# Layer 2's gathers and scatters: one at each of four points of a step, rows fetched two groups ahead, stores a step later, g_init inside VectorE's product

## The chip, the core and the metric

The kernel runs on one core of a Trainium2 chip. Five engines work from their own in-order queues: PE (matrix products), DVE (elementwise work and reductions), ACT (activations and copies), POOL (elementwise work, and here the issue of every indirect DMA) and SP (which issues the plain DMAs). The metric is the time of one execution in microseconds (us); lower is better.

## What is computed

The input x has 32 sequences of 128 tokens with 128 features. Four layers follow; each adds a gated cross-attention over a context and a gated feed-forward part. What the change touches is the end of layer 1 (a mixture of experts), the whole of layer 2, and a preparation for layer 3 that runs beside layer 2:

```python
    # end of layer 1: top-2 mixture over 8 experts, on t = rmsnorm(x1, g2)
    x = x + tanh(g_ffn[1]) * _L1_ffn_ref(_layernorm(x), ...)
    # layer 2: attention, 8 heads of 16; then a top-2 mixture with LayerNorm
    x = x + tanh(g_xattn[2]) * _L2_xattn_ref(ctx_2048, _layernorm(x), mask, b)
    x = x + tanh(g_ffn[2]) * _L2_ffn_ref(_layernorm(x), gamma, beta, Wg, ...)
    # layer 3, the part prepared beside layer 2: a decayed running sum of
    h_patch = rmsnorm(ctx_2048, g_init)[..., :128]      # then picked by patch ends, + h
```

The top-2 mixture is computed by sending: each token's row is stored twice, once into a slot of each of its two experts; each expert works through its slots; each token's two result rows are fetched back, weighted and added to x.

## The kernel before, in words

The 32 sequences are eight groups of four (NG = 8, NB = 4). x stays in SBUF for the whole run as eight tiles of 128 tokens by 4 x 128.

**Stages.** The attention of layers 0, 1 and 1f (the small attention inside layer 1's feed-forward part) runs in one pipeline, up to about 1257 us of the profiled execution. The experts of layer 1 follow, up to 1416. Then layer 2's attention, up to about 1791. Then layer 2's experts, and from about 1987 layer 3.

**A step.** Attention is cut into steps (`Pipe.turn`, lines 434 to 454). Layer 2 has four a group: two sets of four heads, each in two halves of two sequences. A step traces, in this order: the row maxima put into the query stack and the finishing of older outputs (lines 439 to 441); the weights of the part that is four back (`self.todo[0][0]()`, scores transposed and their exponential); the products with the values of the part before that, and at a group's last part its `after`; then

```python
            move(to_fetch, 3)
            move(to_store, 2)
```

(lines 450, 451); then one piece of the oldest `after` in the queue `afters`, if there was one when the step began; then one piece of the work beside (`last_layer`, line 1167). After the step, `run` (line 410) takes one piece of the next group's `before`.

**before(g)** (line 1251) empties `to_fetch`, adds the fetched rows (`routes1.add`, line 833: eight products per group on DVE), takes a LayerNorm (POOL computes the inverse root, line 208), and ends its first piece. Its second piece makes the query parts (line 289: two casts on POOL, lines 301 and 303) and the values (POOL, lines 285, 286), and queues the fetch of the following group's rows: eight indirect DMAs of 128 rows, issued on POOL (line 821), into one of two buffers `got`.

**after(g)** (line 1265) adds the attention's output, takes a LayerNorm with a second scale (POOL, line 254: `w`), and ends its first piece. Further pieces: the router's logits and the top-2 choice (`Routes.take`, line 642, two yields); the last piece appends eight stores to `to_store` (line 705), each an indirect DMA on POOL (line 636) which needs the slot numbers (`slot_r`, line 692). So an `after` has four pieces and a group has four steps. In layer 1f a group has eight steps, its `after` has five pieces, and it uses the same `take` and the same `turn`.

**last_layer** computes, group by group, the root mean square of the context (POOL line 208), multiplies it in on DVE (line 1197) and multiplies by the row `g_init` on POOL (line 1198), before a product with the decay matrix on PE (line 1203).

**flush** (line 456) runs the steps that are left; then, while there are `afters`, it takes a piece of one and a piece of the work beside. `drain` then empties `to_store`.

**Order.** What the program text says is not the order on the engines. The builder's planner lines up each engine's instructions by when it reckons their inputs and buffers to be ready; text order is their priority. An indirect DMA of this kernel is in addition marked with `keep_in_program_order`, which ties it behind the instruction traced before it on POOL. Once lined up, each engine's queue is fixed and runs in order.

Of the kernel before, what the change touches and what calls it, by code (L numbers as in the profile page):

```python
# [22 lines left out]
P = 128  # L23
# [49 lines left out]
def tile_flamingo_gated(  # L73
# [149 lines left out]
    def bc(a, n=D):  # L223
        return a[:, :, None].to_broadcast([a.shape[0], a.shape[1], n])
# [15 lines left out]
                of = of.rearrange("p (h e d) -> p e h d", e=2, d=8)  # L240
            nc.vector.tensor_scalar(to, of, mv[:, b, 0:1], r[:, b : b + 1], ALU.subtract, ALU.mult)  # L241

    def layernorm(pool, a, tag="y", bufs=None, halves=False, again=None):

        mv = moments(pool, a)
        if again:

            w = pool.tile([P, 2, NB], F32, tag="w2", name="w2")  # L250
            nc.vector.tensor_scalar(w[:, 0], mv[:, :, 1], EPS, None, ALU.add)
            nc.vector.tensor_scalar(w[:, 1], mv[:, :, 1], 1.0 + EPS, EPS * EPS, ALU.mult, ALU.add)
            w2 = w.rearrange("p i b -> p (i b)")
            nc.gpsimd.tensor_tensor(w2, w2, m05.to_broadcast([P, 2 * NB]), ALU.pow)
            r, r2 = w[:, 0], w[:, 1]
        else:
            r = rsqrt(pool, mv[:, :, 1])
        y = None
        if tag:
            y = pool.tile([P, NB, D], F32, tag=tag, name="y", bufs=bufs)  # L260
            scaled(y, a, mv, r, halves)
        if not again:
            return y
        h = pool.tile([P, NB, D], F32, tag=again, name="h")
        scaled(h, a, mv, r2)
        return y, h

# [125 lines left out]
    def move(queue, n=None):  # L393
        for do in queue[:n]:
            do()
        del queue[:n]

    class Pipe:


# [33 lines left out]
        def turn(self, ahead):  # L434
            self.place.append(to_place[:])
            to_place.clear()
            place = self.place.pop(0)
            ready = bool(self.afters)
            for do in to_finish + place:
                do()  # L440
            to_finish.clear()
            if len(self.todo) > ahead:
                self.todo[0][0]()
            if self.last:
                _, products, after = self.last
                products()
                if after:
                    self.afters.append(after())
            self.last = self.todo.pop(0) if len(self.todo) > ahead else None
            move(to_fetch, 3)  # L450
            move(to_store, 2)
            if ready:
                self.advance(self.afters)
            self.beside()

        def flush(self):
            while self.todo or self.last:
                self.turn(0)
            for do in to_finish:
                do()  # L460
            to_finish.clear()
            while self.afters:
                self.advance(self.afters)
                self.beside()

        def drain(self):
            self.flush()
# [141 lines left out]
    class Routes:  # L609
# [32 lines left out]
        def take(self, pool, psum, g, logits, rows, gate, eps):  # L642
# [52 lines left out]
            if eps:  # L695
# [3 lines left out]
                self.weight[:, g], tops, gates[:, gate : gate + 1], den[:, None, :].to_broadcast([P, 2, NB]),  # L699
                ALU.mult, ALU.mult,  # L700
            )
            yield
            for b in range(NB):
                for k in range(2):
# [415 lines left out]
    with ExitStack() as outer:  # L1120
# [29 lines left out]
        with ExitStack() as stack:  # L1150
# [16 lines left out]
            def last_layer():  # L1167
# [13 lines left out]
                for g in range(NG):  # L1181
                    bs = slice(g * NB, (g + 1) * NB)
                    hot = pool.tile([P, NB, P], BF, tag="hot", name="hot", bufs=1)
                    nc.vector.tensor_tensor(
                        hot, CST(cst, "iota_s")[:, None, :].to_broadcast([P, NB, P]), bc(ends[:, bs], P), ALU.is_equal,
                    )
                    ck = pool.tile([P, NB, D], F32, tag="ck", name="ck", bufs=1)
                    nc.sync.dma_start(out=ck, in_=ctx_all[bs, :, 0:D].rearrange("b s d -> s b d"))
                    cnt = psum.tile([P, NB], F32, tag="tp", name="cnt")
                    for b in range(NB):  # L1190
                        nc.tensor.matmul(
                            cnt[:, b : b + 1], lhsT=hot[:, b, :], rhs=ones_b[:, 0:1], start=True, stop=True
                        )
                    nc.vector.tensor_scalar(bound[:, bs], cnt, 1.0, None, ALU.min)

                    r = rms_scale(pool, ck, values_of(pool, g))
                    nc.vector.tensor_tensor(ck, ck, bc(r), ALU.mult)
                    nc.gpsimd.tensor_tensor(
                        ck, ck, ROW(row, "g_init")[:, None, :].to_broadcast([P, NB, D]), ALU.mult
                    )  # L1200
                    yield
                    pd = psum.tile([P, NB, D], F32, tag="tp", name="pd")
                    nc.tensor.matmul(flat(pd), lhsT=CST(cst, "decay"), rhs=flat(ck), start=True, stop=True)
                    dep = pool.tile([P, NB, D], F32, tag="dep", name="dep", bufs=1)
                    nc.scalar.copy(dep, pd)

                    pg = psum.tile([P, NB, P], F32, tag="tp", name="pg")
                    for b in range(NB):
                        at = g * NB + b
                        nc.tensor.matmul(  # L1210
                            pg[:, b, :], lhsT=bound[:, at : at + 1].to_broadcast([P, P]), rhs=CBF(cbf, "tri"),
                            start=True, stop=True,
                        )
                    pick = pool.tile([P, NB, P], F32, tag="pick", name="pick", bufs=1)
                    nc.vector.tensor_scalar(flat(pick), flat(pg), -1.0, 0.0, ALU.add, ALU.max)
                    nc.vector.tensor_scalar(flat(pick), flat(pick), float(P - 1), iota_p, ALU.min, ALU.is_equal)
                    yield
                    po = psum.tile([P, NB, D], F32, tag="tp", name="pdp")
                    with_bias(po, "b_in")
                    for b in range(NB):  # L1220
                        nc.tensor.matmul(
                            po[:, b, :], lhsT=pick[:, b, :], rhs=dep[:, b, :], start=False, stop=b == NB - 1,
                            skip_group_check=True,
                        )
                    nc.scalar.copy(dep, po)
                    nc.sync.dma_start(out=depool[g], in_=flat(dep))
                    yield
# [22 lines left out]

            def before(g):
                if g == 0:
                    gots[0] = routes1.fetch(pool, 0)
                move(to_fetch)
                routes1.add(g, gots.pop(g))
                y = layernorm(pool, xs[g], halves=True)
                yield
# [1 line left out]
                va = augmented(pool, values_of(pool, g), 8, 16, "va", nc.gpsimd.tensor_copy)  # L1259
                o = pool.tile([P, NB, D], F32, tag="o", name="o", bufs=3)  # L1260
                at2[g] = q, [ctx_keys[g]], [va], o
                if g + 1 < NG:
                    gots[g + 1] = routes1.fetch(pool, g + 1)

            def after(g):
                add_gated(xs[g], 2, at2.pop(g)[-1])
                y, yn = layernorm(pool, xs[g], tag="y2", bufs=1, again="yn")
                add_gated(xs[g], 6, y)
                yield
                fT = pool.tile([P, NB, P], F32, tag="fT", name="fT", bufs=1)  # L1270
# [267 lines left out]
```

## Time and profile before

| | |
|---|---|
| median of 4 runs | 2203.02 us (2199.84 to 2214.75) |
| the profiled execution's own time | 2206.84 us |
| its span, first to last instruction | 2205.1 us |
| layers 0, 1, 1f with the stores of layer 1 | up to 1256.6 us |
| layer 2's first fetch | 1419.1 us |
| layer 2's last store issued | 1788.6 us |
| indirect fetches in layer 2's attention | 64, of 1006 ns mean on POOL |
| indirect stores in layer 2's attention | 64, of 989 ns mean on POOL |
| POOL's product with g_init | 8, of 1312 ns mean |

The profile is of one execution. A line of groups gives the source line, the engine, the operation, the tiles, the count, the busy time and the mean, and after the bar the idle time of that engine just before such instructions and what ended it. A view of waits says which engine's instruction waited for which, the total, how often, and the longest. The chain of waits follows the work that ended last back from the end of a stretch, and gives each line's share. A timeline has the start, the duration, the engine and line, and in brackets the idle time ahead of the instruction.

### The profile page before, as it was taken

What the parts mean: (1) busy time and instruction counts of PE and PEld (TensorE: products, weight loads), DVE (VectorE), ACT (ScalarE), POOL (GpSimd) and SP (SyncE); (2) the same over time, 40 slices, a digit from 0 to 9 for tenths busy, and PEclk for the clock granted to TensorE, in tenths of its full rate; (3) what the DMA queues carried; (4) which work ended last, traced back from release to release, by engine and by line L of the source; (5) the groups of instructions that cost most, each with busy time, mean ns of one, the idle gap of its engine ahead of it and who ended that gap; (6) DMA issues with size and microseconds to landing.
All of it is one profiled execution on the core that took longest, in us unless ns stands there. A gap on an engine that the chain in (4) does not pass through costs nothing.

```text
span 2205.1 us, 35468 instructions
## 1 busy us (share of the span) xinstructions
PE 1664.3 (75%) x13624; PEld 1007.4 (46%) x13624; DVE 1207.2 (55%) x3480; ACT 894.5 (41%) x1110; POOL 647.8 (29%) x645
## 2 busy tenths in 40 slices
PE   0699998989999999788877399645656549992445
PEld 0454445456666666555445244333534424441223
DVE  7645455375645577677666333366657621113677
ACT  0277565656778655333233133211112114430335
POOL 5101101010100013355554580254554320006430
PEclk9999999999999999977888599867677669995576
DMA  6564558534323342211211144344343123332110
GB/s 207 154 231 161 188 200 274 183 100 126 100 84 100 104 120 73 54 53 53 59 51 48 60 152 150 113 117 136 104 122 116 33 91 122 132 110 72 32 36 19
DMA packets 164536, 244.66 MB, mean 111 GB/s; under 512 B 20560, under 2 KB 102288, under 8 KB 164112
## 3 DMA queue, kind: packets, MB, share of 16 engines
q1 hardware_dynamic: 156176, 225.62, 33.0%
q0 software_dynamic: 8192, 16.79, 2.5%
q8 instruction: 107, 1.75, 0.3%
q14 instruction: 61, 0.50, 0.1%
HBM read 139.74 MB, written 101.24 MB: 109 GB/s over the span
## 4 chain that ended last, share of the span: by engine, by line
PE 39%; POOL 14%; DVE 14%; issue 7%; DMA 3%; ACT 2%; SPq 0%; POOLq 0%; DVEq 0%; ACTq 0%
PE ye L786 5%; POOL got L821 5%; PE av L581 4%; PE ph L1294 4%; POOL by_expert_r L636 4%; PE sct L498 4%; PE sc L498 3%; PE ph L969 3%; PE p L1135 2%; PE tpe L773 2%; PE p L1137 2%; DVE mx L529 1%; DMA got<-by_expert_r,slot_r 1%; PE tp L272 1%; POOL r L208 1%
## 5 line engine op out<-in xcount | busy, mean ns | idle before, releaser
L564 ACT ACTIVATE w<-sct 128x1024 f32<-128x1024 f32 x288 | 292.6, 1024 | 340.1 <-PE sct L498 337.7
L529 DVE TENSOR_REDUCE mx<-sc 128x8 f32<-128x1024 f32 x160 | 194.8, 1219 | 122.6 <-PE sc L498 122.2
L498 PEld LDWEIGHTS <-stack_q 96*128 96x128 bf16 x2560 | 193.1, 109 | 134.3 <-issue 104.6
L821 POOL DMA_INDIRECT got<-by_expert_r,slot_r x128 | 126.7, 990 | 337.6 <-issue 336.5
L534 DVE TENSOR_REDUCE mx<-sc 128x4 f32<-128x1024 f32 x128 | 152.9, 1221 | 132.7 <-PE sc L498 132.2
L581 PE MATMUL av<-w,va 128*9 128x128 f32 (+2 forms) x3584 | 203.2, 295 | 28.1 <-POOL w L567 24.5
L498 PE MATMUL sc<-stack_k,stack_q 96*128 96x128 bf16 x1536 | 144.9, 241 | 51.5 <-DVE mx L529 21.3
L498 PE MATMUL sct<-stack_q,stack_k 128*128 128x128 bf16 (+1 forms) x1536 | 142.7, 237 | 23.7 <-DVE mx L529 15.4
L498 PEld LDWEIGHTS <-stack_k 128*128 128x128 bf16 (+1 forms) x1536 | 112.1, 107 | 79.5 <-issue 76.4
L301 POOL CAST hml<-whole 128x512 bf16<-128x512 f32 (+1 forms) x56 | 37.2, 664 | 352.2 <-ACT whole L300 177.4
L581 PEld LDWEIGHTS av<-w,va 128*9 128x9 f32 (+2 forms) x3584 | 99.8, 94 | 79.7 <-POOL w L567 36.5
L786 PE MATMUL ye<-hid,w 128*128 128x512 f32 x276 | 133.4, 593 | 1.5 <-DVE hid L1140 1.5
L969 PE MATMUL ph<-h,w 128*128 128x512 f32 x256 | 122.7, 606 | 1.8 <-ACT hn L972 0.9
L208 POOL TENSOR_TENSOR r<-r,m 128x4 f32<-128x4 f32 x56 | 57.4, 1025 | 219.6 <-DVE r L207 211.9
L969 PE MATMUL ph<-hn,w 128*128 128x512 f32 x256 | 121.2, 604 | 0.7 <-ACT hn L972 0.7
L498 PE MATMUL sc<-stack_l,stack_q 96*128 96x128 bf16 x1024 | 111.2, 239 | 0.0
L587 ACT COPY ot<-av 128x512 f32<-128x512 f32 x112 | 65.4, 584 | 102.2 <-PE av L581 95.1
L567 POOL TENSOR_SCALAR_AFFINE_SELECT w<-w 128x1024 f32<-128x1024 f32 x64 | 70.6, 1105 | 110.5 <-ACT w L564 110.2
L498 PE MATMUL sct<-stack_q,stack_l 128*128 128x128 bf16 x1024 | 99.0, 235 | 3.3 <-DVE mx L529 3.3
L564 ACT ACT_TABLE_LOAD x72 | 92.4, 1283 | 9.7 <-PE sct L498 8.5
L593 PE MATMUL tpo<-cst,ot 128*128 128x128 f32 x448 | 81.0, 303 | 17.5 <-DVE mrows L550 9.8
L241 DVE TENSOR_SCALAR y<-x,bmv,r 128x128 f32<-128x128 f32 x160 | 48.6, 360 | 73.9 <-POOL r L208 72.0
(288 smaller groups left out, 3312.6 us busy)
## 6 DMA issues: line engine op xcount, KB each, us to landing
by_expert_r<-zeros SPq DMA_DIRECT2D x40, 1024.0 KB
stack_q<-q SPq DMA_DIRECT2D x96, 288.0 KB
stack_k<-k SPq DMA_DIRECT2D x96, 288.0 KB
k<-hml SPq DMA_DIRECT2D x16, 1152.0 KB
w<-in_e_dram SPq DMA_DIRECT2D x23, 514.5 KB
xt<-by_expert_r SPq DMA_DIRECT2D x46, 256.0 KB
by_expert_r<-yt SPq DMA_DIRECT2D x46, 256.0 KB
q<-hml SPq DMA_DIRECT2D x72, 128.0 KB
```

What stands on the lines that cost most here:

```text
L208: nc.gpsimd.tensor_tensor(r, r, m05.to_broadcast([P, NB]), ALU.pow)
L498: nc.tensor.matmul(dst[:, h * P : (h + 1) * P], lhsT=stat[rows, 4 * e + h, b], rhs=mov[rows, 4 * e + h, b], start=start and h == e == 0, s ...
L529: nc.vector.tensor_reduce(mx[:, :, b0 : b0 + 2].rearrange("p h b -> p b h"), sc.rearrange("p i (h k) -> p i h k", h=4), AX.X, ALU.max, neg ...
L534: nc.vector.tensor_reduce(mx[:, :, b0], sc.rearrange("p i (h k) -> p h i k", h=4), AX.XY, ALU.max, negate=True,)
L564: nc.scalar.activation(w.rearrange("p i h k -> p i (h k)"), sc, AF.Exp)
L581: nc.tensor.matmul(av[32 * h : 32 * h + dv + 1, b * P : (b + 1) * P], lhsT=values[c][:, b, 4 * u + h, :], rhs=w[:, i, h, :], start=c == 0, ...
L593: nc.tensor.transpose(tp[:, b].rearrange("p s r -> p (s r)"), ot[:, b, :], ident)
L636: ins = nc.gpsimd.indirect_dma_start(out=self.rows(), out_offset=bass.IndirectOffsetOnAxis(ap=slots, axis=0), in_=rows, in_offset=None,)
L786: nc.tensor.matmul(y, lhsT=w2[:, f, :], rhs=hid[:, f, :], start=f == 0, stop=f == n_f - 1)
L821: ins = nc.gpsimd.indirect_dma_start(out=got[:, k, b, :], out_offset=None, in_=self.rows(), in_offset=bass.IndirectOffsetOnAxis(ap=self.sl ...
L969: nc.tensor.matmul(ph, lhsT=wt[:, c, f * P : (f + 1) * P], rhs=h[:, c, :], start=c == 0, stop=c == 3)
L1294: nc.tensor.matmul(ph, lhsT=E2(w, "w1")[:, f * P : (f + 1) * P], rhs=xT, start=True, stop=True)
```

## The change

- `turn` no longer moves three fetches and two stores together. A new `drip` moves one of the two queues by one; it is called at four points of a step: after the placing, after the weights, after the products and `after`, and at the end. Odd calls prefer a fetch, even ones a store; an empty queue gives its turn to the other. `flush` calls it twice for each piece of an `after` that it takes. Since `turn` is shared, the stores of layer 1f move this way too.
- `take` has one more yield ahead of appending the stores. An `after` of layer 2 has five pieces now, one of layer 1f six.
- Layer 2 fetches rows two groups ahead, into three buffers: group 0's and group 1's at the start, then group g + 2's from `before(g)`. The tile `yn`, from which rows are stored, has three buffers instead of two.
- `last_layer` multiplies by the root mean square and by g_init in one DVE instruction for each of four sequences; POOL's product is gone.

```diff
+    turns = [0]
+    def drip():
+        turns[0] += 1
+        first, other = (to_fetch, to_store) if turns[0] % 2 else (to_store, to_fetch)
+        move(first or other, 1)
...
             to_finish.clear()
+            drip()
             if len(self.todo) > ahead:
                 self.todo[0][0]()
+            drip()
             if self.last:
                 _, products, after = self.last
                 products()
                 if after:
                     self.afters.append(after())
             self.last = self.todo.pop(0) if len(self.todo) > ahead else None
-            move(to_fetch, 3)
-            move(to_store, 2)
+            drip()
             if ready:
                 self.advance(self.afters)
             self.beside()
+            drip()
...
             while self.afters:
                 self.advance(self.afters)
                 self.beside()
+                drip()
+                drip()
...
             yield
+            yield
             for b in range(NB):
                 for k in range(2):
                     to_store.append(...)
...
-                    nc.vector.tensor_tensor(ck, ck, bc(r), ALU.mult)
-                    nc.gpsimd.tensor_tensor(
-                        ck, ck, ROW(row, "g_init")[:, None, :].to_broadcast([P, NB, D]), ALU.mult
-                    )
+                    for b in range(NB):
+                        nc.vector.scalar_tensor_tensor(
+                            ck[:, b, :], ck[:, b, :], r[:, b : b + 1], ROW(row, "g_init"), ALU.mult, ALU.mult
+                        )
...
             def before(g):
                 if g == 0:
-                    gots[0] = routes1.fetch(pool, 0)
-                move(to_fetch)
+                    gots[0] = routes1.fetch(pool, 0, 3)
+                    move(to_fetch)
                 routes1.add(g, gots.pop(g))
...
-                if g + 1 < NG:
-                    gots[g + 1] = routes1.fetch(pool, g + 1)
+                if g == 0:
+                    gots[1] = routes1.fetch(pool, 1, 3)
+                move(to_fetch)
+                if g + 2 < NG:
+                    gots[g + 2] = routes1.fetch(pool, g + 2, 3)
...
-                y, yn = layernorm(pool, xs[g], tag="y2", bufs=1, again="yn")
+                y, yn = layernorm(pool, xs[g], tag="y2", bufs=1, again="yn", again_bufs=3)
```

## The prediction, made before the result was known

> **What bounds the kernel now.** I read the page first, for the engines' shares and the chain that ended last.
>
> ```profile
> span 2205.1 us, 35468 instructions
> PE 1664.3 (75%) x13624; PEld 1007.4 (46%) x13624; DVE 1207.2 (55%) x3480; ACT 894.5 (41%) x1110; POOL 647.8 (29%) x645
> PE ye L786 5%; POOL got L821 5%; PE av L581 4%; PE ph L1294 4%; POOL by_expert_r L636 4%; PE sct L498 4%; PE sc L498 3%; PE ph L969 3%; PE p L1135 2%; PE tpe L773 2%; PE p L1137 2%; DVE mx L529 1%; DMA got<-by_expert_r,slot_r 1%; PE tp L272 1%; POOL r L208 1%
> ```
>
> POOL is busy only 29% of the span, yet its issues of fetches (L821) and stores (L636) hold 9% of the chain. The change acts where they are issued, so I cut layer 2's attention into head, body and tail (busy time by engine, then granted clock, DMA share, GB/s):
>
> ```profile
> 1416.00:1463.00 47.00, 6.80 (x46) 5.32 (x46) 23.38 (x81) 1.19 (x2) 32.16 (x35) 0.52 0.34 98
> 1463.00:1735.00 272.00, 168.79 (x1676) 130.37 (x1677) 178.55 (x698) 50.52 (x69) 125.30 (x131) 0.72 0.39 115
> 1735.00:1797.00 62.00, 21.10 (x208) 15.98 (x207) 28.05 (x141) 6.92 (x11) 26.57 (x26) 0.56 0.15 51
> ```
>
> In the body PE is busy for 169 of 272 us, DVE for 179, POOL for 125. No engine is full: the body is bound by hand-overs between queues. The chain from 1560 to 1665 says which, and DVE's waits in the body and the groups of layer 2's attention give prices:
>
> ```profile
> by line: DMA got<-by_expert_r,slot_r 17.1%; issue 10.0%; POOL by_expert_r L636 8.6%; POOL got L821 7.9%; DVE bst L218 6.0%; POOL w L254 4.8%; POOL r L208 3.9%; POOL ck L1198 3.6%; DVE mx L529 3.2%; DVE y L241 2.9%; DVE h L241 2.9%; PE pdp L
> ...
> DVE x L833 <- DMA got<-by_expert_r,slot_r: 20.3, 12, 4.2
> DVE y L241 <- POOL r L208: 17.5, 5, 6.2
> DVE y L241 <- POOL w L254: 11.3, 6, 4.6
> DVE ck L1197 <- POOL r L208: 5.2, 6, 1.2
> ...
> L833 DVE SCALAR_TENSOR_TENSOR x<-got,weight_r,x 128x128 f32<-128x128 f32 x64 | 22.5, 365 | 27.6 <-DMA got<-by_expert_r,slot_r 27.5
> L1198 POOL TENSOR_TENSOR ck<-ck,row 128x512 f32<-128x512 f32 x8 | 10.5, 1312 | 5.9 <-DVE ck L1197 3.3 <-DVE r L207 1.7 <-DVE bound L1194 0.9
> L1197 DVE TENSOR_TENSOR ck<-ck,r 128x512 f32<-128x512 f32 x8 | 5.9, 740 | 6.1 <-POOL r L208 6.1
> ```
>
> A third of that stretch of chain is a fetch landing, a fetch issued or a store issued. POOL's timeline shows the queueing:
>
> ```profile
> 1648.98 0.97 POOL L821 DMA_INDIRECT got<-by_expert_r,slot_r  x1 [0.30 <-DMA stack_k<-k]
> 1650.26 0.96 POOL L821 DMA_INDIRECT got<-by_expert_r,slot_r  x1 [0.30 <-issue]
> 1651.52 1.00 POOL L636 DMA_INDIRECT by_expert_r<-h,slot_r  x1 [0.30 <-issue]
> 1652.83 0.98 POOL L636 DMA_INDIRECT by_expert_r<-h,slot_r  x1 [0.30 <-issue]
> 1653.84 1.05 POOL L208 TENSOR_TENSOR r<-r,m 128x4 f32<-128x4 f32 x1
> ```
>
> Eleven indirect DMAs run back to back from 1639.4, one each 1.28 us (0.97 and a gap of 0.30); the inverse root for a LayerNorm stands behind them, and DVE waits 6.2 us for it. The program text hands out five DMAs a step; the planner has made eleven of it.
>
> **The change, part by part**, against the profiled execution's own 2206.84 us (span 2205.1 and 1.7 around it), which is 3.8 above the median of the runs.
>
> *Rows fetched two groups ahead.* Removed: DVE's 20.3 us of waits in the body. The other 7.2 of the 27.5 lie in the head, where group 0's rows have nothing ahead of them, and stay. Bounds: all 20.3, or none. None is possible because the adds already run early: the rows of group 6 are added from 1585 to 1605, while the text puts them after a step of group 5 that takes its maxima at 1645. The planner issues an add as soon as it reckons the row landed, and a third buffer lets it do so earlier still. A wait that goes is also partly replaced: DVE idles a third of the body anyway. I take 0.4, -8.
>
> *The issue of those DMAs.* Count and price stay (64 fetches, 64 stores in layer 2), but a lone DMA ahead of an inverse root delays it by at most 1.28. DVE's wait for L208 without a queue is 5.2 / 6 = 0.87; five waits should cost 4.3 and cost 17.5, so 13.2 is queue. For L254, without the 4.6 at 1724.8 which belongs to the tail, 6.7 in five, less 4.3, is 2.4. Queue: 15.6. All of it may go (-15.6). The other end is a gain turned round: fetch and store now alternate, so a fetch and a root may stand behind a store that waits for its slot (POOL stood 31.6 us in four such waits in the body), +10 for one more of the mean 7.9 and a little. The planner bunches again, so I take a third, -5. The new fetch also precedes its add by some three steps, 30 us, so a late fetch itself costs nothing as long as that lead is there; without it the 20.3 are back.
>
> *Stores a step later.* In the tail each group's second LayerNorm waits: its inputs are ready at 1721.9, 1743.5 and 1763.8, and L254 starts at 1724.8, 1746.1 and 1766.3 behind three or more stores: 2.9 + 2.6 + 2.5 = 8.0. Tied further back, the stores should follow L254: I take -5, bounds -8 and +18. The +18 is the backlog: an `after` now has five pieces against four steps a group, and a chain of one `after` is 17.8 long (1761.5 to 1779.3).
>
> *g_init on DVE.* POOL loses 8 x 1.31 = 10.5 of busy time. DVE gets 32 products of the kind of L833 (same size, a scalar per row) for 8 of L1197. Back to back, two L833 take 0.60, so four take 1.12, against 0.69 for L1197 undisturbed: +0.43 a group, +3.4; at 365 ns each it is 8 x (1.46 - 0.74) = +5.8. Two thirds of 3.4 lie on the path, +2. PE waited 14.5 us in three waits for the product with g_init; the path to it loses the 1.26 and a hand-over of 0.2, and the wait is mostly one of 10.6 for a late root. -3, bounds -14.5 and 0. Together -1.
>
> The row bearing on the new DVE work is L833's spread: 327 to 1349 ns, 365 in the mean, so 32 products lose 32 x 0.04 = 1.2 to whatever holds them. The Trainium skill, "SBUF — State Buffer", section "SBUF: two separate sides", speaks against the edit: a DVE instruction with two SBUF inputs and a GpSimd instruction that reads SBUF exclude each other for the whole instruction. If each of the 32 met one L208 of 1.03, the part would be +33 in place of -1. The longest L833 looks like that case (1.0 over the usual), but the mean says that it is rare.
>
> *The head.* Group 1's fetches were already early; with a third buffer eight more (group 3's, 10 us of POOL) may slip in front of POOL's casts before the first scores. 0 to +10; the casts wait mostly for other things, +2.
>
> *Layer 1f.* Its 64 stores go four a step, one at each point, a step later. There a store burst keeps the rotary sum (L1071) waiting: ready at 1098.2, it starts at 1101.2 behind three stores; DVE waits 15.9 in five for it, of which 9.3 is queue. That may go or come again: -9 to +9. Stores are still issued when their slots are reckoned ready, which the change does not move, so 0. On SP nothing is moved; its loads only follow.
>
> Sum: -8 - 5 - 5 - 1 + 2 + 0 = -17. From the median, 2203.0 - 17 = 2186.
>
> **The rivals.** *Nothing happens* (2203, within 11 us): the planner bunches the DMAs as before and puts the adds directly behind the fetches. For it: the eleven in a row, and adds 40 us ahead of their place. Against it: the removed product and the later stores are real. *All of it comes* (2156): 20.3 + 15.6 + 8 = 44, and 3 of PE's wait. For it: all four are on the chain. Against: DVE's busy time in the body is already two thirds. *Slower by the backlog* (2219): the last two groups' `after` both run behind the last products, so the tail grows by a chain of 17.8 and its eight stores, 8 x 1.28 = 10.2, together 28, less the 12 that the other parts bring: +16. For it: five pieces in four steps, falling behind by one a group, and lower priority for what is traced later. Against: the pieces depend on data alone, and the engines in the tail are half idle. It decides from a tail that grows by 23 us (from 57 us between the last row maximum at 1734 and the last store's landing at 1791).
>
> **How the numbers follow.** Forecast (-11 to -35) 0.45; all of it 0.10; nothing 0.20; slower 0.25. I count half a per cent, 11 us, as what a measurement can tell from no change. Faster is 0.55, the same 0.20, slower 0.25. The range reaches to the full gain's 2156 and past the backlog's 2219: 2156 to 2222. The forecast case alone is 2168 to 2192.
>
> **What would show it.** Right: DVE's waits for fetched rows in the body fall below 12 us and those for L208 below 13; L254 in the tail starts within 1 us of its inputs; PE no longer waits for a POOL product ahead of L1203; head and tail each keep their length within 5 us. Wrong: runs of eight and more DMAs on POOL with a root behind them, the last maximum more than 60 us ahead of the last store, or a body that stays at 272 us though the waits for rows are gone, which would mean that another wait took their place. Layer 1f ending more than 9 us away from 1256.6 would show that its stores are not neutral.

## The result, and the profile after

The changed kernel took 2209.38 us in the median (2204.35 to 2218.76, 49 runs) and the kernel before, beside it, 2203.25 us (2189.64 to 2215.58, 75 runs). The ratio is 1.0031, with a 95% interval from 1.0022 to 1.0040: slower by 6 to 7 us, where 17 us less were forecast. By the bound of half a per cent it is "the same", which had 0.20.

Its profiled execution took 2202.89 us (span 2201.1), 6.5 below its own median, while the one of before lay 3.8 above its median. So the two profiles say nothing on the total; they are read for their stages. The stretches of layer 2's attention, cut at the same events as before (first fetch, first row maximum, last row maximum, last store issued; columns: busy time by engine with its count, then granted clock, DMA share, GB/s):

```profile
1414.00:1463.00 49.00, 6.84 (x46) 5.33 (x46) 20.76 (x80) 1.19 (x2) 38.82 (x42) 0.50 0.35 97
1463.00:1717.00 254.00, 160.41 (x1642) 125.70 (x1643) 172.76 (x694) 49.30 (x68) 101.68 (x108) 0.71 0.42 119
1717.00:1785.00 68.00, 21.35 (x236) 16.83 (x235) 30.93 (x165) 7.73 (x12) 34.02 (x34) 0.62 0.09 30
```

The head is 48.6 us (44.2 before), the body 253.9 (270.3), the tail 68.0 (54.9). The body gave 16.4, head and tail took 17.5 of it back. Layer 1f's last store went out at 1252.0 (1256.6 before).

DVE's longest waits in the body, and the chain from 1560 to 1665:

```profile
DVE x L846 <- DMA got<-by_expert_r,slot_r: 21.9, 12, 4.8
DVE y L241 <- POOL w L254: 13.8, 6, 5.6
DVE mx L541 <- PE sc L510: 11.7, 10, 2.8
DVE y L241 <- POOL r L208: 7.7, 4, 2.8
...
by line: DMA got<-by_expert_r,slot_r 9.9%; issue 7.6%; POOL by_expert_r L648 7.0%; DVE mx L541 6.8%; POOL got L834 6.7%; DMA stack_k<-k 6.2%; PE sc L510 4.7%; PE sct L510 4.4%; DVE bst L218 4.3%; POOL w L254 3.2%; SPq L366 3.1%; POOL r L208
```

The waits for fetched rows, which two groups of lead should have ended, are still there: 21.9 us against 20.3. The waits for the inverse root (L208) did fall, from 17.5 to 7.7; those for the second root (L254) rose, from 11.3 to 13.8. POOL's timeline shows how the DMAs stand:

```profile
1577.29 0.98 POOL L834 DMA_INDIRECT got<-by_expert_r,slot_r  x1 [0.30 <-issue]
1578.58 0.98 POOL L648 DMA_INDIRECT by_expert_r<-h,slot_r  x1 [0.30 <-issue]
1579.86 0.98 POOL L834 DMA_INDIRECT got<-by_expert_r,slot_r  x1 [0.30 <-issue]
...
1601.72 0.98 POOL L648 DMA_INDIRECT by_expert_r<-h,slot_r  x1 [14.56 <-DVE negp L167]
1603.01 0.96 POOL L834 DMA_INDIRECT got<-by_expert_r,slot_r  x1 [0.30 <-issue]
1604.28 0.98 POOL L648 DMA_INDIRECT by_expert_r<-h,slot_r  x1 [0.30 <-issue]
1605.56 0.96 POOL L834 DMA_INDIRECT got<-by_expert_r,slot_r  x1 [0.30 <-issue]
```

Fetch and store really alternate. They do not spread over a step, though: they still run back to back, in runs of at most seven in the body (eleven before), and at 1601.72 a store waits 14.56 us with two fetches behind it. Nor do the adds follow later: matched in order, an add starts in the median 6.9 us after the issue of its fetch, where it was 5.9 before.

In the tail POOL's timeline reads:

```profile
1721.97 1.03 POOL L648 DMA_INDIRECT by_expert_r<-h,slot_r  x1 [18.73 <-DVE slot_r L704]
...
1730.92 0.97 POOL L648 DMA_INDIRECT by_expert_r<-h,slot_r  x1 [0.30 <-issue]
1731.91 1.66 POOL L254 TENSOR_TENSOR w<-w,m 128x8 f32<-128x8 f32 x1
1745.98 1.32 POOL L648 DMA_INDIRECT by_expert_r<-h,slot_r  x1 [12.40 <-DVE slot_r L704]
...
1756.24 1.66 POOL L254 TENSOR_TENSOR w<-w,m 128x8 f32<-128x8 f32 x1
```

All eight stores of a group stand ahead of the next group's L254, which was to be freed of them, and after the last L254 sixteen stores follow in place of thirteen. DVE's waits for L254 in the tail, before and then after:

```profile
DVE y L241 <- POOL w L254: 8.5, 2, 4.3
...
DVE y L241 <- POOL w L254: 13.9, 2, 7.7
```

Last, the groups on DVE that the change touches, and PE's wait for the product with g_init, which comes from DVE now:

```profile
L846 DVE SCALAR_TENSOR_TENSOR x<-got,weight_r,x 128x128 f32<-128x128 f32 x64 | 20.8, 347 | 29.5 <-DMA got<-by_expert_r,slot_r 29.4
L1211 DVE SCALAR_TENSOR_TENSOR ck<-ck,r,row 128x128 f32<-128x128 f32 x32 | 9.3, 349 | 8.9 <-POOL r L208 8.9
...
PE pd L1216 <- DVE ck L1211: 9.9, 2, 7.3
```

Two more waits ahead of those matmuls, of 5.8 and 0.7 us, the profile does not put down to that product: PE is idle ahead of them for 16.4 us in all, where it was 14.5 before.

### The profile page after: what moved, and what is told of

Its sections match the earlier page's. It is cut to its first block, busy times and chain, and to the rows that moved or that the text cites. A ratio compares the mean times of both kernels' runs of the same rounds, so it can differ in the third digit from the quotient of the medians.

```text
span 2201.1 us, 35488 instructions
## 1 busy us (share of the span) xinstructions
PE 1647.1 (75%) x13624; PEld 997.1 (45%) x13624; DVE 1196.9 (54%) x3504; ACT 894.2 (41%) x1110; POOL 640.5 (29%) x637
## 4 chain that ended last, share of the span: by engine, by line
PE 40%; POOL 15%; DVE 14%; issue 5%; DMA 3%; ACT 2%; SPq 0%; POOLq 0%; ACTq 0%; DVEq 0%
PE ye L799 5%; POOL got L834 5%; POOL by_expert_r L648 4%; PE av L593 4%; PE ph L1310 4%; PE sct L510 4%; PE ph L982 4%; PE sc L510 4%; DVE mx L541 2%; PE p L1148 2%; PE tpe L786 2%; PE p L1150 2%; POOL w L579 1%; POOL w L254 1%; POOL r L208 1%
## 5 line engine op out<-in xcount | busy, mean ns | idle before, releaser
L510 PE MATMUL sct<-stack_q,stack_k 128*128 128x128 bf16 (+1 forms) x1536 | 136.7, 232 | 22.6 <-DVE mx L541 13.0
L208 POOL TENSOR_TENSOR r<-r,m 128x4 f32<-128x4 f32 x56 | 57.5, 1026 | 211.3 <-DVE r L207 165.4
L579 POOL TENSOR_SCALAR_AFFINE_SELECT w<-w 128x1024 f32<-128x1024 f32 x64 | 70.2, 1098 | 111.2 <-ACT w L576 110.9
L1310 PE MATMUL ph<-xT,w 128*128 128x512 f32 x184 | 87.8, 620 | 0.8 <-DVE nx L727 0.8
```

What stands on the lines that cost most here:

```text
L510: nc.tensor.matmul(dst[:, h * P : (h + 1) * P], lhsT=stat[rows, 4 * e + h, b], rhs=mov[rows, 4 * e + h, b], start=start and h == e == 0, s ...
L579: nc.gpsimd.affine_select(out=heads, in_=heads, pattern=[[0, 8], [1, P]], compare_op=ALU.is_ge, fill=0.0, base=0, channel_multiplier=-1,)
L1310: nc.tensor.matmul(ph, lhsT=E2(w, "w1")[:, f * P : (f + 1) * P], rhs=xT, start=True, stop=True)
```

## The experiments

Kernels sent together ran on one chip, beside the kernel before; the chips differ, the kernel before took 2203 to 2219 us on them, so a ratio to it counts, and times compare only among kernels that ran together. This table holds what the verdicts rest on; stretches are from each kernel's one profile (layer 1f from its first to its last store issued), and "rows" is DVE's wait in the body that the profile puts down to fetched rows. Ahead of the same adds it shows further idle time without a releaser, above 2 us in four kernels: 4.4 us in e2, 8.8 in e4, 9.9 in e11 and 7.0 in e17.

| kernel | ratio to before, 95% | layer 1f | head | body | rows | tail |
|---|---|---|---|---|---|---|
| before (two profiles) | 1 | 302.5, 299.9 | 44.2, 44.4 | 270.3, 285.6 | 20.3, 15.2 | 54.9, 55.8 |
| changed | 1.0031 (1.0022 to 1.0040) | 302.4 | 48.6 | 253.9 | 21.9 | 68.0 |
| e1 no extra yield | 1.0019 (0.9995 to 1.0043) | 304.1 | 48.7 | 278.0 | 15.1 | 56.5 |
| e2 no single moves | 0.9924 (0.9902 to 0.9947) | 296.7 | 49.4 | 253.7 | 12.3 | 66.4 |
| e3 one group ahead | 1.0022 (0.9997 to 1.0046) | 311.0 | 43.5 | 282.5 | 36.8 | 62.9 |
| e4 g_init on POOL | 1.0014 (0.9991 to 1.0037) | 304.5 | 49.6 | 266.6 | 13.9 | 67.4 |
| e5 changed | 1.0021 (1.0004 to 1.0038) | 309.9 | 48.7 | 256.2 | 23.1 | 68.1 |
| e6 single moves alone | 1.0007 (0.9993 to 1.0022) | 304.1 | 44.4 | 265.6 | 22.8 | 59.4 |
| e7 rows and g_init alone | 0.9993 (0.9974 to 1.0013) | 293.4 | 49.3 | 268.1 | 20.7 | 56.6 |
| e8 single moves in 1f only | 0.9971 (0.9953 to 0.9989) | 303.2 | 49.3 | 248.1 | 15.4 | 66.1 |
| e9 no single moves | 0.9913 (0.9882 to 0.9943) | 294.3 | 49.4 | 253.9 | 15.9 | 66.5 |
| e10 extra yield alone | 0.9934 (0.9909 to 0.9960) | 296.7 | 44.3 | 265.8 | 20.9 | 68.9 |
| e11 single moves in 2 only | 0.9926 (0.9899 to 0.9952) | 294.3 | 48.6 | 255.5 | 16.2 | 67.8 |
| e12 single moves in 1f alone | 1.0008 (0.9987 to 1.0028) | 304.2 | 44.4 | 285.3 | 17.1 | 57.0 |
| e13 changed | 1.0009 (0.9992 to 1.0026) | 306.0 | 48.6 | 255.3 | 23.8 | 68.0 |
| e14 no single moves | 0.9921 (0.9893 to 0.9950) | 293.5 | 49.3 | 247.2 | 15.5 | 66.1 |
| e15 single moves in 1f only | 0.9976 (0.9958 to 0.9994) | 303.2 | 49.3 | 247.8 | 18.6 | 66.1 |
| e16 single moves in 2 only | 0.9979 (0.9961 to 0.9997) | 293.7 | 48.5 | 258.1 | 31.4 | 68.0 |
| e17 fetches in threes | 1.0017 (0.9995 to 1.0039) | 305.1 | 49.3 | 259.9 | 9.3 | 67.1 |

### First set: one part undone at a time

My first theory was the tail: five pieces of an `after` on four steps push stores behind the last products, and the body's gain is given back there. Four kernels each undo one part of the changed kernel.

```diff
 # e1: one yield in take
-            yield
...
 # e3: one group ahead, two buffers
+                    gots[g + 1] = routes1.fetch(pool, g + 1)
...
 # e2: drip() gone from turn and flush; in turn, at the old place
+            move(to_fetch, 3)
+            move(to_store, 2)
...
 # e4: the root on DVE, then g_init on POOL
+                    nc.vector.tensor_tensor(ck, ck, bc(r), ALU.mult)
+                    nc.gpsimd.tensor_tensor(ck, ck, ROW(row, "g_init")..., ALU.mult)
```

> The changed kernel with one yield ahead of the stores, as before; the other three parts stay. Theory A (the stores' delay gives the gain back in the tail: five pieces of an after on four steps, group 6's eight stores left behind group 7's): the stretch from the last row maximum to the last store issued, 68.0 us with the change and 54.9 before it, returns to 55 to 60, at most 13 stores stand behind the last inverse root instead of 16, and the time falls by 8 to 13 us, to 2196 to 2201. Theory B (body and tail are one account: the last maximum came 16 us earlier only because work was pushed behind it): the body takes back what the tail gives, first to last maximum 262 to 270 us instead of 253.9, and the time stays at 2209 within 4.

> The changed kernel with three fetches and two stores moved together at one point of a step, as before; the other parts stay. Theory A: the single moves shortened the body, so the body goes from 253.9 us back to some 262 and the tail stays at 66 to 70: 2214 to 2219. Theory B: the planner orders the DMAs by readiness whatever the text says, so body and tail both stay within 4 us and the time at 2209 within 4. My forecast priced this part at -5, so undone at +5.

> The changed kernel with rows fetched one group ahead into two buffers, as before; the other parts stay. My forecast priced the part at -8, less +2 in the head, so undone it is +6: 2215, with VectorE's waits for fetched rows in layer 2 at 27 us or more. Theory A and B agree on the head: 48.6 us from the first fetch to the first maximum fall back to 44 to 45. If the third buffer did nothing but that, as VectorE's unchanged wait of 29.4 us for rows says, the time is 2205 within 3 and the waits stay at 27 to 30.

> The changed kernel with the product with g_init on GpSimd again, eight instructions of 1.31 us; the other parts stay. My forecast priced the part at -1: undone 2210, within 3. Rival: 32 more products on VectorE beside a busy GpSimd hold each other up, at most 33 us: undone 2195 or less. Second rival: the order of everything on GpSimd shifts with the eight instructions and the difference is that of the order, 2203 to 2216, with body and tail moving against each other.

Medians: e1 2218.65, e2 2196.32, e3 2217.97, e4 2217.18, the kernel before 2214.06 us. The tail theory falls: without the extra yield the tail is 56.5 us as it said, with thirteen stores behind the last root, but the body takes it all back (278.0) and the time does not fall. Neither does it fall when rows or g_init are put back. Only the single moves matter, and with the sign opposite to every expectation: undone, the kernel is 0.76% below the kernel before, where the changed kernel, on other chips, was 0.31% above it: together 1.07%, some 23 us.

### Second set: the changed kernel again, and parts alone

```diff
 # e6: before, with drip() in turn and flush       # e5: the changed kernel
 # e7: before, with fetch(pool, g + 2, 3) and the product of four sequences on DVE
 # e8: the changed kernel, drip() only while layer 1f runs
+        if routes1.done:
+            return
...
+            if routes1.done:
+                move(to_fetch, 3)
+                move(to_store, 2)
```

> The changed kernel itself, beside the others on one chip, for its stages. Theory C (single moves cost, the other three parts earn): 0.2 to 0.4% above the kernel before, layer 1f's last store at 1252 to 1257 us against 1245.5 without the single moves, body of layer 2 (first to last maximum) 262 to 275 us against 253.7. Theory D (the kernel without single moves was a lucky order in one place): the changed kernel's stages equal those of the kernel without single moves but for one.

> The kernel before with the single moves alone. Theory C: slower than before by about what their removal from the changed kernel gained, 0.8 to 1.2%. Theory D, or parts that only cost together: within 0.4% of before. My forecast had -5 us, -0.2%.

> The kernel before with rows two groups ahead and g_init on VectorE, neither single moves nor the later stores. If these two hold the gain of 0.76% that the changed kernel without single moves shows, the ratio to before is 0.990 to 0.995; by my forecast's terms (-8, -1, +2 in the head) it is -7 us, 0.997. If the later stores carry the gain: 0.998 to 1.002.

> The changed kernel with single moves in layer 1f only; layer 2 moves three fetches and two stores at one point as before. If the cost of the single moves lies in layer 1f: ratio to before 1.000 to 1.004 and last store of layer 1f at 1251 or later. If it lies in layer 2's body: ratio 0.990 to 0.995 and body at 254 to 258 us. If half each, 0.996 to 0.999.

Medians: 2205.79, 2205.11, 2200.93, 2196.54, the kernel before 2205.15 us. Rows two groups ahead and g_init on DVE together are worth nothing that can be measured (e7), so the later stores must hold the gain that e2 showed. Single moves added to the kernel before cost nothing (e6): theory C's 0.8 to 1.2% fails. They cost when the stores come later: without the later stores the kernel with single moves is at 1.0019 (e1) and the one with the old moves at 0.9993 (e7); with the later stores the two are at 1.0021 (e5) and 0.9924 (e2). The changed kernel's body is 256.2 us, below what theory C expected. Giving back the old moves in layer 2 alone (e8) brings 0.5%: body 248.1.

### Third set: the later stores alone

```diff
 # e9: as e2                    # e11: the changed kernel, drip() only in layer 2
 # e10: before, with one more yield in take and again_bufs=3
 # e12: before, with drip() only while layer 1f runs
```

> The changed kernel without single moves once more, on the chip of the three that follow. Theory E (the single moves cost twice, some 10 us in layer 1f and some 8 in layer 2): ratio to before 0.990 to 0.995, last store of layer 1f at 1243 to 1249 us. If 0.9924 was that chip's: 0.997 or more, as with single moves in layer 1f only.

> The kernel before with the stores' later piece alone (one more yield, a third buffer for the rows stored). Theory E, with the gain in layer 1f that the single moves take away: layer 1f's last store 6 to 10 us earlier than the kernel before has it, tail of layer 2 longer by some 10 (66 us), ratio 0.996 to 1.001. Rival: the later stores only cost, tail 66 us and layer 1f as before, ratio 1.003 to 1.006. My forecast had -5 us, 0.998.

> The changed kernel with single moves in layer 2 only; layer 1f moves two stores at one point as before. Theory E: it keeps layer 1f's gain (last store at 1243 to 1249) and pays in layer 2 (first fetch to last store 370 to 374 us against 363.5 with single moves in 1f only), ratio 0.996 to 0.999. If layer 2's part of the cost was chance, the ratio is that of the kernel without single moves, 0.990 to 0.995.

> The kernel before with single moves in layer 1f only, no later stores. If single moves cost in layer 1f by themselves: ratio 1.003 to 1.006. If they only take away what the later stores gain there: ratio 0.999 to 1.001 and the last store of layer 1f within 3 us of the kernel before.

Medians: 2198.54, 2205.53, 2202.14, 2221.66, the kernel before 2219.45 us. The extra yield alone gives 0.66% here, more than was expected of it: its tail is 68.9 us, as long as the changed kernel's, but layer 1f takes 296.7 in place of some 302, and body and tail together 334.7 where e12, which has layer 2 in the order of before, took 342.3 on the same chip. e11's 0.9926 said that single moves in layer 2 cost next to nothing (3.6 us above e9, inside the intervals), where the chip of e5 and e8 had given 9.3: the two disagreed, and the question stayed open.

### Fourth set: the two-by-two table on one chip

e13 is the changed kernel, e14 has the edit of e2, e15 that of e8, e16 that of e11.

> The changed kernel: single moves in both layers. Theory E (the loss lies in layer 1f): 8 to 12 us above the kernel without single moves and the one with single moves in layer 2 alone; last store of layer 1f at 1252 to 1259 us. Theory F (both layers): 16 to 20 us above the kernel without single moves, half of it in the stretch of layer 2's attention (370 to 374 us against 364 to 370).

> The changed kernel without single moves. Both theories: the fastest of the four or equal to the fastest, 0.7 to 1% below the kernel before; last store of layer 1f at 1245 to 1247, layer 2's attention 369 to 370 us.

> Single moves in layer 1f alone. Theory E: equal to the changed kernel within 4 us. Theory F: 8 to 10 us below the changed kernel, 8 to 10 above the one with single moves in neither.

> Single moves in layer 2 alone. Theory E: within 4 us of the kernel without single moves, layer 1f's last store at 1245 to 1248. Theory F: half way between the changed kernel and the one without single moves.

| median, us | layer 2: old moves | layer 2: single moves |
|---|---|---|
| layer 1f: old moves | 2185.86 (e14) | 2198.52 (e16) |
| layer 1f: single moves | 2199.44 (e15) | 2205.14 (e13) |

The kernel before took 2205.38 us. Theory F holds in the sum (16 to 20 us expected), less well in the halves: single moves cost 13.6 and 6.6 us in layer 1f, 12.7 and 5.7 in layer 2, 19.3 together. The other three parts earn 19.5 us. (The intervals of the ratios are 4 us to each side, 6 for e14; so each single difference is known to some 5 to 7 us, the two sums are well clear of zero.) The change is the sum of the two: nothing on this chip, +0.31% where it was first measured.

*Layer 2.* DVE's waits for rows in the body, first with single moves (e13), then without (e14):

```profile
DVE x L846 <- DMA got<-by_expert_r,slot_r: 23.8, 11, 4.7
...
DVE x L842 <- DMA got<-by_expert_r,slot_r: 15.5, 8, 4.4
```

The difference of 8.3 us is near that of the bodies, 255.3 against 247.2. With the idle time that has no releaser, the changed kernel, e5, e11, e13 and e16 wait 21.9 to 31.4 us ahead of these adds, and e2, e8, e9, e14 and e15, with the old moves in layer 2, 15.4 to 18.6. POOL's timeline of e13 around 1606, with the slot number and the add on DVE, the next scores on PE, and the root that follows on POOL:

```profile
1605.25 0.17 DVE L704 CAST slot_r<-t_slot 128x8 int32<-128x8 f32 x1
1605.69 0.98 POOL L648 DMA_INDIRECT by_expert_r<-h,slot_r  x1 [15.48 <-DVE negp L167]
1606.98 0.96 POOL L834 DMA_INDIRECT got<-by_expert_r,slot_r  x1 [0.30 <-issue]
1608.24 0.98 POOL L648 DMA_INDIRECT by_expert_r<-h,slot_r  x1 [0.30 <-issue]
1609.53 0.96 POOL L834 DMA_INDIRECT got<-by_expert_r,slot_r  x1 [0.31 <-issue]
...
1610.36 0.35 DVE L846 SCALAR_TENSOR_TENSOR x<-got,weight_r,x 128x128 f32<-128x128 f32 x1 [4.66 <-DMA got<-by_expert_r,slot_r]
1610.63 1.22 DVE L541 TENSOR_REDUCE mx<-sc 128x8 f32<-128x1024 f32 x1
...
1611.90 1.44 PE L510 MATMUL sc<-stack_k,stack_q 96*128 96x128 bf16 x12 [5.00 <-DVE mx L541]
...
1615.38 1.04 POOL L208 TENSOR_TENSOR r<-r,m 128x4 f32<-128x4 f32 x1 [2.33 <-DVE r L207]
```

and the same place of e14:

```profile
1598.62 0.16 DVE L700 CAST slot_r<-t_slot 128x8 int32<-128x8 f32 x1
1599.06 1.33 POOL L644 DMA_INDIRECT by_expert_r<-h,slot_r  x1 [12.83 <-DVE negp L166]
1600.69 0.99 POOL L644 DMA_INDIRECT by_expert_r<-h,slot_r  x1 [0.30 <-issue]
1601.99 0.96 POOL L644 DMA_INDIRECT by_expert_r<-h,slot_r  x1 [0.30 <-issue]
1603.26 0.97 POOL L644 DMA_INDIRECT by_expert_r<-h,slot_r  x1 [0.30 <-issue]
...
1605.86 1.04 POOL L208 TENSOR_TENSOR r<-r,m 128x4 f32<-128x4 f32 x1 [0.35 <-DVE r L207]
```

In both a store waits 13 to 15 us for its slot number (the profile names a `negp` instruction that ran just beside it, but the store starts 0.27 and 0.28 us after the end of DVE's write of `slot_r`). With three fetches and two stores moved together the fetches had gone ahead of it. Moved singly, two of them stand behind it. The planner had put the adds right behind the fetches, so DVE waits 4.66 us, with a row maximum behind that wait, and PE waits 5.00 for that maximum. In the five profiles of the changed kernel, e5, e11, e13 and e16 an add waits 4.7 to 5.0 us at this place; in e2, e8, e9, e14 and e15, which have the old moves in layer 2, none does.

What the place costs is less than these waits. Up to the write of `slot_r` the bodies of e13 and e14 are equal (it comes 139.3 and 139.7 us after the first row maximum); from it to the next root (L208) e13 takes 10.1 us and e14 7.2. So 2.9 of the 8.1 us are lost here, and the rest later. In the next stretch, up to the row maxima at 1644.12 in e13 and 1631.34 in e14, 3.3 more are lost; there a root stands behind five alternating DMAs in e13 and behind three in e14, and DVE waits for it, in e13 and then e14:

```profile
1643.80 0.41 DVE L241 TENSOR_SCALAR y<-x,bmv,r 128x128 f32<-128x128 f32 x1 [2.83 <-POOL r L208]
...
1630.17 0.35 DVE L241 TENSOR_SCALAR y<-x,bmv,r 128x128 f32<-128x128 f32 x1 [0.94 <-POOL r L208]
```

From the write of `slot_r` to the last row maximum the five with single moves take 115.5 to 117.0 us, the others 107.4 to 111.2, but e9 114.0.

*Layer 1f.* No fetch is issued there. DVE's waits for POOL, from first to last store, with single moves (e13), then without (e14):

```profile
DVE t L1110 <- POOL r L208: 14.7, 7, 2.9
DVE rest L302 <- POOL hml L301: 13.3, 9, 2.5
DVE hml L304 <- POOL hml L303: 9.5, 10, 1.6
DVE rt L1079 <- POOL rt L1084: 2.2, 1, 2.2
...
DVE hml L304 <- POOL hml L303: 8.4, 8, 1.6
DVE t L1106 <- POOL r L208: 4.4, 5, 1.2
DVE rest L302 <- POOL hml L301: 4.0, 10, 1.2
```

In e14 the long waits are gone, 16.8 us against 39.7 in these lines, and the stretch is 293.5 us against 306.0. The order on POOL of one group, read from the queues (s a store, m a mask on the weights):

```
before   s m s s s s rt m hml s rt hml   m hml s va hml m s m   m r
changed  s m s s s   rt m hml s rt hml s m hml s va hml s m m   m r
e14      s m s s s   rt m hml s rt hml   m hml s va hml m s m s m r
```

The changed kernel takes one store away from the rotary sum `rt`, as was hoped, and puts it ahead of a mask and a cast (`hml`), for which DVE then waits (L302). With the old moves the late stores fall between masks, where POOL waits for ACT anyway (3.63 us ahead of the one at 1112.94 in e14), and the roots come with fewer waits. The casts are shown by the order; that the roots' 10 us have the same cause is only argued, since a mask stands right ahead of the root in both. The stretch itself is clear over all profiles: with the later stores it takes 302.4 to 311.0 us in the eight profiles with single moves in layer 1f, and 293.5 to 296.7 in the six with the old moves.

### Fifth set: which of the two single moves

```diff
 # e17: the changed kernel; drip() moves stores only, on the turns it had
+        if turns[0] % 2 == 0 or not to_fetch:
+            move(to_store, 1)
...
+            move(to_fetch, 3)
             drip()
             if ready:
 # e18: the kernel before, for a second profile
```

> The changed kernel with the fetches moved three together at one point of a step and the stores still singly. Theory G (the single fetch costs in layer 2: its landing is late, and VectorE waits 23.8 us for rows in the body against 15.5 without single moves): the waits for rows fall to 15 to 19, the body to 247 to 251 us, and the ratio to before is that of single moves in layer 1f alone, 0.996 to 0.999. Theory H (the single store costs): waits and body as in the changed kernel, 22 to 25 and 254 to 258 us, ratio 1.000 to 1.003.

> The kernel before, for a second profile of its stages. If an unchanged order of layer 1f ends in one of two places, its 64 stores spread over 293 to 296 us here or over 302 to 304; the first profile has 302.5. No theory foretells which; body 268 to 286 us, tail 55 to 57.

Medians: e17 2217.91, e18 2217.02 (one run), the kernel before 2215.75 us. Theory G falls as I had put it: e17's waits that the profile gives to rows go down to 9.3 us (16.3 with a wait of 7.04 that it gives to nothing), yet body and ratio stay those of the changed kernel. Its POOL and DVE timelines show the same jam:

```profile
1604.31 1.01 POOL L649 DMA_INDIRECT by_expert_r<-h,slot_r  x1 [10.54 <-DVE slot_r L705]
1605.62 0.98 POOL L649 DMA_INDIRECT by_expert_r<-h,slot_r  x1 [0.30 <-issue]
1606.91 0.98 POOL L835 DMA_INDIRECT got<-by_expert_r,slot_r  x1 [0.30 <-issue]
1608.20 0.97 POOL L835 DMA_INDIRECT got<-by_expert_r,slot_r  x1 [0.30 <-issue]
1609.48 0.95 POOL L835 DMA_INDIRECT got<-by_expert_r,slot_r  x1 [0.30 <-issue]
...
1613.90 1.43 DVE L847 SCALAR_TENSOR_TENSOR x<-got,weight_r,x 128x128 f32<-128x128 f32 x4 [7.04 <-issue]
```

Three fetches behind the waiting store, and DVE idle for 7.04 us before the add (the profile names no releaser, but the add follows the fetches). From the write of `slot_r` to the next root e17 takes 20.4 us, 13 more than e14, as much as its body is longer (12.7, on another chip). So the single fetch is not needed for the jam: fetches behind a store whose slot number is not written yet are enough. The stores were still moved singly in e17, and no kernel moved fetches singly and stores in twos, so theory H, that the single store costs, is not refuted: its ratio came, its waits for rows did not. Nor is the jam the whole of the 6 to 13 us in layer 2: in e13 it is 2.9 of 8.1, a root behind alternating DMAs some 2 more, and the rest is open.

## Why the prediction was wrong

The sum was -17. The step on the single issue had the wrong sign and measured +19 in two places; the others brought what I had summed for them and more, though not where I had put it. And the sum added terms that are not independent: alone, single moves cost nothing (e6).

*Issue of the DMAs singly, -5 (bounds -15.6 and +10).* This is the step that failed. It measured +5.7 and +12.7 in layer 2 on the chip of the table, +9.3 and +3.6 on two others. About half of the queue that I priced (15.6) went: waits for L208 fell from 17.5 to 7.7 us, those for L254 rose by 2.5. But the other end, "a fetch and a root may stand behind a store that waits for its slot", which I had put in as a bound of +10, is what the profiles show: DVE and PE stand 5 us for fetches behind such a store. I leaned on a lead that did not exist: "the new fetch also precedes its add by some three steps, 30 us". The profile before had shown that adds run early, directly behind the fetches; I had written so in the paragraph above, and should have taken no lead beyond theirs (6.9 us in the median with the change, 5.9 before). I also expected the planner to bunch as before; it alternated the DMAs, still without gaps, in shorter runs.

*Layer 1f, 0 (bounds -9 and +9).* Single moves cost 6.6 and 13.6 us there in the presence of the later stores. The stretch took 302.4, 309.9 and 306.0 us in three profiles of the change, 302.5 and 299.9 in two of before. Against these two the later stores by themselves seem to bring 3 to 6 (e10: 296.7), but e7, without them, took 293.4, so that gain is not shown. As far as zero was right, it was luck: a cost stood in the place that I had priced at nothing.

*Stores a step later, -5 in the tail.* Place and sign in the tail were wrong: the waits of DVE for L254 there went from 8.5 to 13.9 us, and the tail grew by 13.1 in place of shrinking. Yet this part carries the gain. e8 and e7, which ran together, differ in layer 2 only in it: the body goes from 268.1 to 248.1 us and the tail from 56.6 to 66.1. A backlog it is, as the rival said, but it takes work from the body that it puts in the tail, so a grown tail alone was no test of slower. Alone, with the old moves, this part is worth -0.66% (e10).

*Rows two groups ahead, -8 (bounds -20.3 and 0).* The bound of none came. The waits for rows did not go, and undoing the part (e3) or adding it with g_init (e7) leaves the time alone, though in e3 the waits rise to 36.8 us.

*g_init on DVE, -1.* Undone (e4) the time stays, as a part of -1 should. The cost came as priced: the group on DVE takes 9.3 us against 5.9, the +3.4 of the text. The -3 on PE is not shown: its idle time ahead of the product with the decay matrix went from 14.5 to 16.4 us. The new products take 349 ns in the mean and 395 at most, the adds 347 and 415. The longest add of before, 1349 ns at 1461.04, did not meet a root, as I had guessed, but POOL's product with g_init (from 1460.59 to 1462.23). The runs bear that out: the longest add of layer 2's attention takes 1349 to 1353 ns in each of the six profiles with that product on POOL (before, e4, e6, e10, e12, e18), and in the fourteen without it 362 to 535, once 814 (e3). The Trainium skill, "SBUF — State Buffer", section "SBUF: two separate sides", says that a DVE instruction with two SBUF inputs and a GpSimd (POOL) instruction that reads SBUF hold each other off for the whole instruction. The adds beside POOL's product agree with that; adds beside a root do not: in e7 one of 0.35 us ran from 1537.75, inside a root from 1537.63 to 1538.67, and e9 and e16 show the same. So the +33, a whole root for each product, is not borne out. The 32 new products did not meet the case: in the profile of the changed kernel they run beside DMA issues and beside no other instruction of POOL.

*The head, +2.* It is +4.4, inside its bounds; all kernels that fetch two groups ahead have 48.5 to 49.6 us, all others 43.5 to 44.4.

Measured by the two-by-two table, the parts other than single moves brought -19.5 us where I had summed -12, and single moves +19.3 where I had -5. The rival "nothing happens" named the right time and half of the mechanism: the adds again stand directly behind the fetches, but the DMAs were not bunched as before, and the time stayed because a gain and a cost cancel, which was luck. Of the signs, the waits for L208 fell below 13 as for right, those for rows did not fall below 12, and the last row maximum came 68.0 us ahead of the last store, a sign of wrong.

The version without single moves beats both kernels: 0.9921 (0.9893 to 0.9950) on one chip, 0.9913 and 0.9924 on two others.

## What to carry to other kernels

Before a queue that several producers share is interleaved more finely, ask for each kind of entry what it waits for: an entry whose input is late holds everything behind it, and here a burst that kept the ready entries ahead of it was better than an even mix. A lead written into the text counts only if the consumer's place moves too; here the adds stayed some 7 us behind their fetches. Prices of parts do not add when one part moves what another waits for. And a stretch that shrinks may only have pushed its work into the next one, so compare stretches together, and parts of a change in all combinations on one chip before naming the one that costs.

## What was not expected of the hardware

The same order of instructions in layer 2 took 270.3 us for the body in the first profile of before and 285.3 (e12) and 285.6 (e18) on other chips. The body of e18:

```profile
1457.00:1743.00 286.00, 181.31 (x1660) 138.13 (x1661) 177.28 (x695) 49.76 (x68) 125.37 (x131) 0.66 0.39 109
```

DVE and POOL are busy as long as in the first profile (177.28 and 125.37 us; 178.55 and 125.30 there), but PE takes 181.3 us in place of 168.8, at a granted clock of 0.66 in place of 0.72. The profile's slices of that stretch read 0.5 to 0.8 over the runs. So two profiles of one order can differ by 15 us in this stretch, the longer one at the lower clock, and a longer body in one profile alone does not show a worse order. The changed kernel without single moves (e2, e9, e14) had 0.71 to 0.73 and 247 to 254 us on three chips. Whether fewer gaps on PE hold the clock up, or a held clock makes the gaps shorter, these runs do not tell. Layer 1f, too, took 293.4 us in e7 and 302.5 and 299.9 in the kernel before, though the order on POOL and DVE is the same there; the granted clock was 0.80 in e7 and 0.76 and 0.78 in the kernel before. That spread of 9 us is as large as what a part of this change does; what sets the clock is left open.
